# Four graph layers on one core: table writes moved to ScalarE's queue, and new times for the stages of a woven schedule

## The chip, the cores and the metric

The kernel runs on one core of a Trainium2 chip. The time is the device time of one execution in microseconds (us); smaller is better. Three runs of the kernel before gave 3189.59, 3191.43 and 3202.73 us, so the median is 3191.43 us. One more execution was taken with the hardware profiler; all durations below are from it.

Names of engines: PE is TensorE (matrix multiply; PEld is its weight load), DVE is VectorE, ACT is ScalarE, POOL is GpSimd, SP is SyncE, which here only issues DMAs. PSUM is the memory that PE writes into; SBUF is the working memory.

## What is computed

`x` is 32 items of 512 nodes with 256 features; `adj` is one 512x512 matrix with few entries that are not zero, shared by all items. Four layers follow each other. Layers 0 and 3 have the same form:

```python
pre_u = h @ W1[:d];  pre_v = h @ W1[d:]
hidden = relu(pre_u[:, :, None, :] + pre_v[:, None, :, :] + b1)
S = sigmoid(hidden @ W2 + b2)                 # one number per pair of nodes
a = einsum('buv,bud->bvd', S * adj, h)
m = einsum('uv,bud->bvd', adj, h) * h
z = beta1*h + beta2*(a @ Wa + ba) + beta3*(m @ Wm + bm)
```

Layer 1 is `z + relu((adj @ z) @ W.T + b)`. Layer 2 is a dense attention over all 512 nodes: features, one logit per node, softmax of leaky_relu(f_i + f_j) + adj, weighted sum, plus the input.

`S * adj` is zero wherever `adj` is, so the kernel computes `S` only for the pairs of nodes that have an edge.

## The kernel before, in words

The 32 items are worked in 8 groups of 4 (`NB = 4`, group number `t` = 0 to 7). For each group there are five kinds of work. Each is a Python generator, and each `yield` ends one *piece*:

- **first** (29 pieces): for each item load `x` (SP), transpose it on PE (L664) and copy it out on ACT (L665), write the transpose to DRAM (ACT's queue, L898), compute `m` on PE and DVE (`mhT`, L880) and store it (SP, L902), and then `pre`.
- **pre** (4 pieces per item, inside `first` and inside `middle`): two matmuls per piece (L678, L680) give `pre_u` and `pre_v` for 128 nodes. DVE copies one half out of PSUM with the bias (L683), ACT copies the other half (L686), DVE makes a small sum (L688). The result `puv` (128 x 512 numbers, 256 KB) is written to the group's table in DRAM (L692). `puv` has three buffers.
- **edges** (50 pieces; once for layer 0 and once for layer 3 of each group): 40 *turns*. Each turn gathers 128 rows of the table with an indirect DMA (POOL, L717), DVE combines them with the rows of the other end of the edges (L811 to L813), ACT (L797) or DVE (L831) sums them, then come exp (ACT, L702), the rest of the sigmoid and the factor `adj` (DVE), and an indirect DMA scatters the values into a dense matrix in DRAM, `cells` (POOL, L711). Four fetches run ahead of the turns, and five pieces of leftover scatters follow them.
- **middle** (about 120 pieces): load the dense `S * adj` of layer 0 (`SA`, POOL, L857), lay it out with ACT (`flat`, L944), the rest of layer 0 (L972, L979), layer 1 (L993 and `adjT,zW`), layer 2 (L1015, softmax L1039 to L1045, transposes L1084, `eT,feats`), and `pre` for layer 3. Its transposed result goes to DRAM as `x2T` (SP, L1064).
- **last** (33 pieces): for each item the products `hWa` and `mhT` of layer 3 (2 pieces each), the sums over the dense `S * adj` of layer 3 (2 pieces, L1133), the `Wm` product (2 pieces, L1142), and the store of the output (SP).

All of it is emitted into one program by `weave`. `sparse_path` gives every piece of every stream a time; one unit of time is one *turn of the groups*, and `middle` of group `t` fills the times from t - 0.47 to t + 0.53 (cut off at zero; the last two groups have some numbers of their own). `weave` sorts all pieces by time and emits them in that order, with one exception: `first` and `last` are "fill" streams. Their pieces wait in a list and are emitted only where a piece of `middle` yields True, a *room*: a place where PE would have to wait for another engine. One piece, or two if the list is long, goes into each room; more than 8 are never held back. `middle_shares` sets how much of a turn each piece of `middle` takes; so it sets which edge turns and which fill pieces come between which pieces of `middle`. PE executes nearly in the order of emission; a scheduler shifts some instructions of the other engines.

In times, a turn looks like this before the change (phase 0 is the start of a `middle`): edges of layer 3 of the group before from 0.003 to 0.54, edges of layer 0 of the group after from 0.448 to 0.96, `last` of the group before from 0.56 to 1.13, which reaches into the next turn. `first` of group t + 1 stands from 0.14 to 0.40 of the turn of group t, just before the edges of layer 0 that read its table. Group 2 is an exception: its `first` runs from 0.1 to 0.45 beside the `middle` of group 0. So the `middle` of group 1 has no `first` beside it.

The table write is held back by one piece. `pre` stores it as a closure in `self.later`, and the next piece of `pre`, of whichever stream, issues it on SP's queue through `settle`; the ends of `first` and `middle` call `settle` too:

```python
self.settle()
self.later = lambda c=c, puv=puv: nc.sync.dma_start(rows[:, c, :, b, :], puv)
yield
```

Of the kernel before, what the change touches and what calls it, by code (L numbers as in the profile page):

```python
# [19 lines left out]
NC = N // P  # L20
DC = D // P
G = 32
NB = 4
# [494 lines left out]
class Sparse:  # L518
# [3 lines left out]
    def __init__(self, ctx, m, counts, xr, outr, B):  # L522
        self.m, self.nc, self.tc, self.counts = m, m.nc, m.tc, counts
        tc = m.tc
        self.xr, self.outr = xr, outr
        pool = lambda n, b, **k: ctx.enter_context(tc.tile_pool(name=n, bufs=b, **k))
        self.dram = pool("dram", 1, space=bass.MemoryType.DRAM)

        self.cells = {
            k: [self.dram.tile([CELLS + SPARE, NB], F32, name=f"cells_{k}{q}") for q in range(2)] for k in "03"  # L530
        }
        self.lists = self.dram.tile([N, 2 * N], F32, name="lists")
        self.x2s = self.dram.tile([B, P, NC, D], F32, name="x2s")

        self.xT, self.x2T = (self.dram.tile([B, P, DC, N], F32, name=n) for n in ("xT", "x2T"))
        self.mhTs = self.dram.tile([B, P, DC, N], F32, name="mhTs")
        self.e = Edges(m, pool("edges", 1))
        self.adjT = pool("adjT1", 1).tile([P, NC, N], F32, name="adjT")
        self.grp = pool("grp", 2)
        self.act, self.small, self.gath = pool("act", 1), pool("small", 2), pool("gath", 6)  # L540
        self.ps = pool("ps", 7, space=PSUM)
        self.ps_f1 = pool("ps_f1", 1, space=PSUM)
        self.later, self.bigs, self.given, self.marks = None, 0, None, {}

    def psum(self):
        return self.ps.tile([P, N], F32, name="pst", tag="pst")
# [121 lines left out]
    def pre(self, g, b, hT):  # L668

        nc, w = self.nc, g.w  # L670
        rows = g.table.rearrange("(c p k) (b d) -> p c k b d", p=P, k=2, b=NB)
        for c in range(NC):
            cs = slice(c * P, (c + 1) * P)
            if c % 2 == 0:
                two = [self.psum() for _ in range(2)]
                for k, pp in enumerate(two):
                    ks = slice((c + k) * P, (c + k + 1) * P)
                    nc.tensor.matmul(pp, hT[:, 0, ks], w["W1"][:, 0::DC, :], start=True, stop=False)  # L678
            pp = two[c % 2]
            nc.tensor.matmul(pp, hT[:, 1, cs], w["W1"][:, 1::DC, :], start=False, stop=True)  # L680
            puv = self.small.tile([P, 2, D], F32, name="puv", bufs=3)
            part, mixed = (g.parts[:, k, c, b : b + 1] for k in range(2))
            nc.vector.scalar_tensor_tensor(  # L683
                puv[:, 0, :], pp[:, 0:D], 1.0, w["bu"], ALU.mult, ALU.add, accum_out=part
            )
            nc.scalar.copy(puv[:, 1, :], pp[:, D:])  # L686
            junk = self.small.tile([P, MIXED.stop - MIXED.start], F32, name="mixed", bufs=1)
            nc.vector.scalar_tensor_tensor(  # L688
                junk, puv[:, 0, MIXED], 1.0, w["sign"][:, 0, :], ALU.mult, ALU.mult, accum_out=mixed
            )  # L690
            self.settle()
            self.later = lambda c=c, puv=puv: nc.sync.dma_start(rows[:, c, :, b, :], puv)  # L692
            yield

    def settle(self):

        if self.later:
            self.later()
        self.later = None

    def exp_of(self, w, t):
        self.behind(self.nc.scalar.activation(t, t, AF.Exp, bias=w["nb2"], scale=-1.0))  # L702
# [182 lines left out]
    def first(self, g, i):  # L885


        def load(b):
            h = self.act.tile([P, NC, D], F32, name="h0", tag="h", bufs=2)
            self.nc.sync.dma_start(h, self.xr[i + b])  # L890
            return h

        h = load(0)
        for b in range(NB):
            ahead = load(b + 1) if b < NB - 1 else None
            hT = self.turned(h, "hT0", "hT")
            yield
            self.nc.scalar.dma_start(self.xT[i + b], hT)  # L898
            if i > 0:
                for mhT in self.mhT(h, hT, 3):  # L900
                    yield
                self.nc.sync.dma_start(self.mhTs[i + b], mhT)  # L902
            yield from self.pre(g, b, hT)
            h = ahead
        self.settle()

    def middle_before(self, g0, i):

# [14 lines left out]
    def middle(self, g0, g3, i):  # L923


        SA = self.load(g0, 0)
        given, self.given = self.given, None
        mhT, hT = self.fresh(i, given)
        hT = hT()
        hWa = None  # L930
        if not given:
            for hWa in self.hWa(g0, hT, 0):
                yield
        flat = self.flat(SA, 0)
        for b in range(NB):
            keep = [mhT, hT, hWa, flat]
            yield from self.middle_one(g0, g3, b, i + b, SA, keep, given)
            mhT, hT, hWa, flat = keep
        self.settle()

    def flat(self, SA, b):
        flat = self.act.tile([P, NC, N], F32, name="flat", tag="eT")
# [236 lines left out]
def spread(shares, a, b):  # L1179

    times, at = [], 0.0
    for share in shares:
        times.append(a + (b - a) * at / sum(shares))
        at += share
    return times


def edge_times(ahead, a, b, behind, lead=LEAD):

    step = (b - a) / TURNS  # L1190
    first = [ahead + j * min(step, (a - ahead) / lead) for j in range(lead)]
    return first + spread(even(TURNS), a, b) + spread(even(TAIL), b, behind)


def middle_shares(given):


    hWa = [] if given else [1.7, 1.7]
    shares = list(hWa)
    for b in range(NB):  # L1200
        more = hWa if b < NB - 1 else []
        shares += [3.4, 3.4, 1.0, 2.7]
        shares += [1.7, 3.4, 2.8, 4.5] + [0.9] * NC
        shares += [0.4, 0.4, 0.4, 1.0, 0.4, 1.0] + more + [1.5, 1.5]
        shares += [2.8, 4.5] + [0.4] * NC + [0.5, 0.5]
    return shares + [0.1]


@with_exitstack
def sparse_path(ctx, m, counts, xr, outr, B):  # L1210


    sp = Sparse(ctx, m, counts, xr, outr, B)
    last = B // NB - 1
    streams = [
        (sp.setup(), spread(even(NC + 1 + NC + 2 * (OWN // 2 + 1) + 1), -0.40, -0.295), ""),
        (sp.setup_behind(), spread(even(2 * (OWN // 2 + 1) + 2 * PANELS + 4), -0.285, -0.16), ""),
        (sp.setup_rest(), spread(even(8), -0.26, -0.20), ""),
        (sp.zeros_behind(), spread(even(2), 0.15, 0.2), ""),
    ]  # L1220
    for t in range(last + 1):
        g0, g3 = Group(sp, m.g0, f"0_{t}"), Group(sp, m.g3, f"3_{t}")
        start, end = (max(0.0, k - 0.47) for k in (t, t + 1))

        if t == 0:
            first = spread(even(NB * 5 + 1), -0.385, -0.30)
            edges0 = edge_times(-0.292, -0.27, -0.03, -0.02, LEAD_AT_ENDS)
        elif t == 1:
            first = spread(FIRST, -0.28, -0.06)
            edges0 = edge_times(0.02, 0.07, start - 0.06, start - 0.04)  # L1230
        else:
            first = spread(FIRST, 0.1, 0.45) if t == 2 else spread(FIRST, start - 0.86, start - 0.6)
            edges0 = edge_times(start - 0.552, start - 0.505, start - 0.06, start - 0.04)
        edges3 = edge_times(end + 0.003, end + 0.05, end + 0.48, end + 0.54)
        behind = end + 0.56, end + 1.13
        if t == last - 1:
            edges3 = edge_times(end + 0.003, end + 0.05, end + 0.46, end + 0.5)
            behind = end + 0.7, end + 1.06
        if t == last:
            end -= 0.2  # L1240
            edges3 = edge_times(end + 0.003, end + 0.02, end + 0.45, end + 0.46, LEAD_AT_ENDS)
            behind = end + 0.29, end + 0.45
        streams += [
            (sp.first(g0, t * NB), first, "fill"),
            (sp.edges(g0, ("yT", "mhT0", "hWa0") if t == 0 else ()), edges0, ""),
            (sp.middle(g0, g3, t * NB), spread(middle_shares(t == 0), start, end), "main"),
            (sp.edges(g3, ("yT", "h1", "hT1") if t == last else ()), edges3, "free"),
        ]
        if t == 0:
            streams.append((sp.middle_before(g0, 0), spread(AHEAD, -0.15, -0.03), ""))  # L1250
        if t < last:
            streams.append((sp.last(g3, t * NB), spread(LAST, *behind), "fill"))
        else:
            streams.append((sp.last_before(g3, t * NB), spread(AHEAD, *behind), ""))
            streams.append((sp.last_behind(g3, t * NB), spread(BEHIND, end + 0.5, end + 0.6), ""))
    sp.weave(streams)
# [237 lines left out]
```

## Time and profile before

| | |
|---|---|
| median of 3 runs | 3191.43 us |
| the profiled execution | 3192.99 us |
| its span, first to last instruction | 3190.9 us |
| mean granted TensorE clock | 0.933 |
| PE / DVE / POOL / ACT busy | 2746.0 / 2110.6 / 1590.5 / 1338.4 us |
| mean busy share of PEld | 52% |
| mean DMA rate | 228 GB/s |

The profiled execution lies 1.6 us above the median. A line of the profile's groups reads: source line, engine, operation, output<-inputs, shapes, count, then busy time and mean duration of one in ns, then the idle time of the engine just before these instructions and what ended it. A table by stretches gives, for each stretch of the span, the busy time of each engine with the number of instructions, then the mean granted PE clock (1.00 is full) and the DMA engines' busy share. A line of the waits reads: who waited <- for whom, total us, number of waits, longest. PE's fp32 matmuls appear as two records each.

### The profile page before, as it was taken

How to read it: one execution, taken by the hardware profiler on the slowest of the kernel's cores; microseconds unless marked ns; L12 is line 12 of the kernel's file. 1: busy time of each engine (PE TensorE's matmuls, PEld its weight loads, DVE VectorE, ACT ScalarE, POOL GpSimd, SP SyncE). 2: the span in 40 equal slices, each digit the busy share in tenths (PEclk: the TensorE clock that was granted, in tenths of full speed). 3: DMA queues.
4: the chain of work that ended last, by engine and by line, in shares of the span. 5: the costliest groups of instructions: out<-in, count | busy, mean ns of one | idle time of the engine just before them, and what ended most of it. 6: DMA issues, size and time to landing. Idle time of an engine off the chain costs nothing.

```text
span 3190.9 us, 32573 instructions
## 1 busy us (share of the span) xinstructions
PE 2746.0 (86%) x8729; PEld 1659.2 (52%) x8730; DVE 2110.6 (66%) x5601; ACT 1338.4 (42%) x4185; POOL 1590.5 (50%) x1535
## 2 busy tenths in 40 slices
PE   6756998769998898988999899998999889979948
PEld 3423444435664555545665456545655456535627
DVE  6752665877577775776767675877757775773651
ACT  4432543544344442544344443544434443443330
POOL 2562443666454564546635464546635564460360
PEclk9887998879999999999999899999999899989979
DMA  7874766677677766786578866786678766652763
GB/s 245 314 218 160 263 203 210 205 238 242 199 258 263 265 225 225 241 286 216 183 263 259 283 212 229 233 269 244 221 241 270 256 227 213 203 192 90 243 200 112
DMA packets 308607, 727.39 MB, mean 228 GB/s; under 512 B 58048, under 2 KB 161472, under 8 KB 300224
## 3 DMA queue, kind: packets, MB, share of 16 engines
q0 software_dynamic: 136128, 448.24, 43.2%
q1 hardware_dynamic: 153904, 240.30, 22.2%
q10 hardware_dynamic: 18384, 36.71, 3.1%
q8 instruction: 70, 1.15, 0.1%
q14 instruction: 121, 0.99, 0.1%
HBM read 564.28 MB, written 160.83 MB: 227 GB/s over the span
## 4 chain that ended last, share of the span: by engine, by line
PE 51%; DMA 20%; DVE 14%; issue 7%; POOL 5%; ACT 3%; POOLq 0%; ACTq 0%; DVEq 0%; SPq 0%
PE pst L49 22%; DMA rows<-table,iv 8%; PE pst L1133 5%; PE pst L678 4%; PE pst L680 4%; PE pst L972 4%; DMA cells<-s,cell 4%; DMA table<-puv 3%; DVE rows L811 3%; PE pst L993 3%; PE pst L1015 2%; POOL cells L711 2%; PE pst L1142 2%; DVE s L831 2%; DVE rows L813 2%
## 5 line engine op out<-in xcount | busy, mean ns | idle before, releaser
L711 POOL DMA_INDIRECT cells<-s,cell x640 | 716.5, 1120 | 845.3 <-DMA cells<-s,cell 524.4
L717 POOL DMA_INDIRECT rows<-table,iv x552 | 597.6, 1083 | 490.1 <-issue 142.3
L797 ACT ACTIVATE rows<-rows 128x256 f32<-128x256 f32 x1160 | 468.9, 406 | 672.7 <-DVE rows L813 359.4
L811 DVE TENSOR_TENSOR rows<-rows,mine 128x576 f32<-128x576 f32 x616 | 462.5, 751 | 324.1 <-DMA rows<-table,iv 301.6
L49 PE MATMUL pst<-adj,h 128*128 128x512 f32 x1024 | 456.0, 592 | 2.4 <-ACT puv L686 2.4
L49 PE MATMUL pst<-L_gnn_Wa,hT 128*128 128x256 f32 x1024 | 277.7, 424 | 139.9 <-DMA hT<-x2T 55.2
L831 DVE TENSOR_REDUCE s<-rows 128x4 f32<-128x1024 f32 x326 | 394.9, 1211 | 2.8
L813 DVE TENSOR_TENSOR rows<-rows,mine 128x448 f32<-128x448 f32 x616 | 379.8, 617 | 0.0
L49 PEld LDWEIGHTS pst<-L_gnn_Wa,hT 128*128 128x128 f32 x1024 | 217.3, 217 | 189.1 <-issue 49.8
L49 PEld LDWEIGHTS pst<-adj,h 128*128 128x128 f32 x1024 | 191.7, 190 | 219.9 <-issue 215.0
L49 PE MATMUL pst<-eT,feats 128*128 128x512 f32 x512 | 251.5, 648 | 31.5 <-ACT eT L1085 31.5
L683 DVE SCALAR_TENSOR_TENSOR puv<-pst,L_gnn_bu 128x256 f32<-128x256 f32 x256 | 106.2, 418 | 242.5 <-DMA table<-puv 137.1
L49 PE MATMUL pst<-adjT,zW 128*128 128x512 f32 x512 | 231.5, 604 | 15.4 <-ACT zW L997 15.4
L1133 PE MATMUL pst<-hWa,SA 128*128 128x256 f32 x896 | 218.3, 399 | 3.1 <-DMA SA<-cells 3.1
L1133 PEld LDWEIGHTS pst<-hWa,SA 128*128 128x128 f32 x896 | 213.7, 328 | 10.3 <-DMA SA<-cells 4.2
L797 ACT ACTIVATION_READ_ACCUMULATOR rows<-rows 128x1 f32 x1160 | 218.1, 188 | 0.0
L686 ACT COPY puv<-pst 128x256 f32<-128x256 f32 x256 | 92.2, 371 | 299.6 <-DVE puv L683 289.6
L944 ACT COPY flat<-SA 128x512 f32<-128x512 f32 x128 | 137.4, 1122 | 182.5 <-DMA SA<-cells 104.1
L972 PE MATMUL pst<-flat,hWa 128*128 128x512 f32 x448 | 197.9, 593 | 2.8 <-ACT hWa L870 2.8
L49 PEld LDWEIGHTS pst<-eT,feats 128*128 128x128 f32 x512 | 104.4, 208 | 163.7 <-issue 124.4
L1084 PE MATMUL pst<-ident,ex 128*128 128x128 f32 x512 | 91.0, 318 | 106.4 <-DVE ex L1045 63.6
L993 PE MATMUL pst<-WT,hT 128*128 128x256 f32 x512 | 136.4, 423 | 45.7 <-DVE hT L980 41.1
(216 smaller groups left out, 4103.5 us busy)
## 6 DMA issues: line engine op xcount, KB each, us to landing
table<-puv SPq DMA_DIRECT2D x256, 256.0 KB, 5.2
SA<-cells POOLq DMA_DIRECT2D x64, 1024.0 KB, 7.1
mine<-table SPq DMA_DIRECT2D x64, 512.0 KB, 6.3
rows<-table POOLq DMA_DIRECT2D x64, 512.0 KB, 5.2
h<-in_x_dram SPq DMA_DIRECT2D x36, 512.0 KB, 5.2
hT<-xT SPq DMA_DIRECT2D x36, 512.0 KB, 4.8
h<-x2s SPq DMA_DIRECT2D x36, 512.0 KB, 3.7
xT<-hT ACTq DMA_DIRECT2D x32, 512.0 KB, 5.3
```

The source lines that it names most:

```text
L49: nc.tensor.matmul(out, lhsT, rhs, start=(n == 0), stop=(n == len(pairs) - 1))
L678: nc.tensor.matmul(pp, hT[:, 0, ks], w["W1"][:, 0::DC, :], start=True, stop=False)
L711: self.nc.gpsimd.indirect_dma_start(out=g.cells[half], out_offset=bass.IndirectOffsetOnAxis(ap=at, axis=0), in_=s, in_offset=None)
L717: self.nc.gpsimd.indirect_dma_start(out=rows, out_offset=None, in_=g.table, in_offset=bass.IndirectOffsetOnAxis(ap=at, axis=0))
L797: self.behind(nc.scalar.activation(part, part, AF.Identity, accum_out=g.s[:, k, b : b + 1]))
L811: self.behind(nc.vector.tensor_tensor(rows[:, :, first], rows[:, :, first], other[:, :, first], ALU.max))
L813: self.behind(nc.vector.tensor_tensor(rows[:, :, behind], rows[:, :, behind], other[:, :, behind], ALU.min))
L831: nc.vector.tensor_reduce(g.s[:, k, :], rows, AX.X, ALU.add)
L944: self.nc.scalar.copy(flat[:, r, :], SA[r][:, :, b])
L972: nc.tensor.matmul(pz, hWa[:, r, cs], flat[:, r, :], start=(r == 0), stop=False)
L993: nc.tensor.matmul(pw[:, at], zT[:, d, cs], m.WT_1[:, d, :], start=(d + k == 0), stop=(d * k == 1))
L1133: nc.tensor.matmul(pz[:, k * D : (k + 1) * D], SA[r][:, cs, b], hWa[:, r, :], start=(r + k == 0), stop=False)
```

## The change

Three things change.

1. The table write is issued from ACT's queue, in the same piece as the copy, and no longer held back. `later` and `settle` go.
2. `first` of the groups 3 to 7 moves from 0.86 .. 0.6 before the group's `middle` to 1.95 .. 1.52 before it: one turn earlier, and over a longer stretch (0.43 in place of 0.26). Group 2 starts at 0.08 in place of 0.1. Groups 0 and 1 keep their times.
3. `middle_shares` and the times of edges and `last` get new numbers. In the shares, the pieces that end in a room and those of the softmax and of `pre` take more of a turn; the split of the four softmax pieces is laid out anew.

The list of items in `Edges.order` is not edited.

```diff
-            self.settle()
-            self.later = lambda c=c, puv=puv: nc.sync.dma_start(rows[:, c, :, b, :], puv)
+            nc.scalar.dma_start(rows[:, c, :, b, :], puv)
             yield
...
     for b in range(NB):
-        more = hWa if b < NB - 1 else []
-        shares += [3.4, 3.4, 1.0, 2.7]
-        shares += [1.7, 3.4, 2.8, 4.5] + [0.9] * NC
-        shares += [0.4, 0.4, 0.4, 1.0, 0.4, 1.0] + more + [1.5, 1.5]
-        shares += [2.8, 4.5] + [0.4] * NC + [0.5, 0.5]
+        more = 0.0 if given or b == NB - 1 else 1.7
+        shares += [3.4, 3.4, 1.0, 3.8]
+        shares += [1.7, 4.5, 2.7, 5.5, 0.9, 0.9, 0.9, 3.7]
+        shares += [1.5, 1.5, 1.5, 2.5, 1.5, 2.5]
+        for _ in range(2):
+            shares += [more] if more else []
+            shares += [2.5]
+        shares += [2.7, 5.5] + [1.0] * NC + [0.8, 0.8]
...
-            first = spread(FIRST, 0.1, 0.45) if t == 2 else spread(FIRST, start - 0.86, start - 0.6)
-            edges0 = edge_times(start - 0.552, start - 0.505, start - 0.06, start - 0.04)
-        edges3 = edge_times(end + 0.003, end + 0.05, end + 0.48, end + 0.54)
-        behind = end + 0.56, end + 1.13
+            first = spread(FIRST, 0.08, 0.45) if t == 2 else spread(FIRST, start - 1.95, start - 1.52)
+            edges0 = edge_times(start - 0.54, start - 0.495, start - 0.06, start - 0.04)
+        edges3 = edge_times(end + 0.003, end + 0.045, end + 0.485, end + 0.52)
+        behind = end + 0.54, end + 1.05
```

More of the change, by code (lines that the diff above doesn't have):

```diff
@@ L542, in __init__ @@
         self.ps_f1 = pool("ps_f1", 1, space=PSUM)
-        self.later, self.bigs, self.given, self.marks = None, 0, None, {}
+        self.bigs, self.given, self.marks = 0, None, {}
     def psum(self):
@@ L690, in pre @@
             )
-            self.settle()
-            self.later = lambda c=c, puv=puv: nc.sync.dma_start(rows[:, c, :, b, :], puv)
+            nc.scalar.dma_start(rows[:, c, :, b, :], puv)
             yield
[L695 to L699, printed above, removed]
     def exp_of(self, w, t):
@@ L904, in first @@
             h = ahead
-        self.settle()
     def middle_before(self, g0, i):
@@ L938, in middle @@
             mhT, hT, hWa, flat = keep
-        self.settle()
     def flat(self, SA, b):
```

## The prediction

> **What bounds the kernel now.** I read the page first: PE is busy 2746.0 of 3190.9 us, far above DVE (2110.6), so some 445 us without PE are the reserve. Then I asked for stretches cut where PE starts a `middle` and where it starts the `last` that goes with it. "Turn k" is the `middle` of group k; its first half has the edges of layer 3, its second those of layer 0.
>
> ```profile
> core 0: us, PE busy (x) PEld busy (x) DVE busy (x) ACT busy (x) POOL busy (x), PEclk, DMA share, GB/s
> 533.00:703.00 170.00, 119.11 (x344) 67.08 (x343) 123.44 (x309) 80.69 (x255) 104.43 (x93) 0.84 0.71 223
> 703.00:865.00 162.00, 144.87 (x490) 95.56 (x488) 116.60 (x283) 67.11 (x213) 93.31 (x87) 0.95 0.67 228
> ...
> 1231.00:1427.00 196.00, 189.94 (x584) 107.45 (x585) 141.05 (x389) 92.86 (x286) 96.86 (x91) 0.97 0.80 264
> 1427.00:1601.00 174.00, 146.20 (x490) 95.22 (x489) 117.10 (x283) 67.17 (x213) 102.97 (x93) 0.94 0.63 213
> ...
> 2324.00:2526.00 202.00, 189.63 (x585) 106.91 (x586) 142.09 (x391) 92.31 (x284) 99.79 (x93) 0.97 0.79 257
> 2526.00:2692.00 166.00, 145.13 (x489) 93.99 (x487) 115.93 (x282) 66.52 (x211) 97.17 (x91) 0.96 0.65 219
> ```
>
> Rows one and two are turn 1, the next two turn 3, the last two turn 6. Turns 2 to 6 look alike: a first half of 196 to 202 us in which PE is busy 188 to 190, so PE bounds it; a second half of 163 to 174 us with PE busy 146, so some 20 us of waits. Turn 1 has no `first`: its first half takes 170 us with PE busy 119, and I read 170 as what the edges alone need. PE's waits in turn 3, first half, then second:
>
> ```profile
> PE pst L49 <- ACT puv L686: 7.9, 1, 7.9
> PE pst L49 <- ACT eT L1085: 3.4, 1, 3.4
> PE pst L1084 <- DVE ex L1045: 1.8, 1, 1.8
> ```
>
> ```profile
> PE pst L49 <- ACT puv L686: 11.4, 1, 11.4
> PE pst L678 <- DVE yT L1062: 4.5, 1, 4.5
> PE pst L1084 <- DVE ex L1045: 3.7, 2, 3.3
> PE pst L993 <- DVE hT L980: 3.5, 2, 2.1
> PE pst L1133 <- DMA SA<-cells: 2.0, 1, 2.0
> ```
>
> The longest is the border between turns: ACT has a `flat` copy that waits for the last `SA` load ahead of the `puv` copies, and PE gets no PSUM tile. The softmax (ex, eT) waits where no fill piece stood in the room.
>
> **Part 1: `first` a turn earlier, `last` sooner.** The PE groups of one turn (1231 to 1600.6) price the fill:
>
> ```profile
> L49 PE MATMUL pst<-adj,h 128*128 128x512 f32 x128 | 57.2, 592 | 0.0
> ...
> L1133 PE MATMUL pst<-hWa,SA 128*128 128x256 f32 x128 | 31.4, 400 | 2.0 <-DMA SA<-cells 2.0
> ...
> L1142 PE MATMUL pst<-L_gnn_Wm,mhT 128*128 128x256 f32 x64 | 15.4, 381 | 0.4 <-DVE mhT L880 0.4
> L680 PE MATMUL pst<-w_L_gnn_W,hT 128*128 128x512 f32 x32 | 15.9, 592 | 0.0
> L678 PE MATMUL pst<-w_L_gnn_W,hT 128*128 128x512 f32 x32 | 15.0, 592 | 0.0
> ```
>
> `first` is half of row one (the other half is `last`'s) plus L678, L680 and the transposes L664 (4.1): 28.6 + 15.0 + 15.9 + 4.1 = 63.6 us of PE. `last` has eight pieces of each kind: sums 31.4/8 = 3.9, `Wm` 15.4/8 = 1.9, `mhT` 28.6/8 = 3.6, `hWa` 2.1 by its row in the same answer.
>
> The order of the two built programs shows what moves. `first` leaves turn 6 and enters turn 1; turns 2 to 5 keep one, of another group. Pieces 23 to 31 of each `last` stood in the next turn's first half; now 27 to 31 do. So 23 to 26 (1.9 + 2.1 + 2.1 + 3.6 = 9.7 us) go to the second half.
>
> - Turns 2 to 5, first half: 9.7 us less PE where PE bounds: -9.7. Bounds: 0 (edges late next) to -9.7.
> - Second half: 9.7 us more PE beside 20 us of waits. Most of those (border, yT, hT) stand where no piece goes, so I let 7 stay: +7. Bounds 0 to +9.7.
> - Turn 1, first half: PE 119.1 falls to 103 at the clock of the full turns (0.84/0.97) and rises by 63.6; with their 9.5 us of waits 176, without any clock gain 192. I take 183: +13 (bounds +6 to +22). Second half as above.
> - Turn 6, first half: no `first`; 202 becomes turn 1's 170 and a little for the 15 us of `last` left: 172, -30 (bounds -32 to -20).
> - Turn 7 (2692 to 2932): 9.7 us of PE less beside some 36 us of gaps: -3 (0 to -9.7).
>
> **Part 2: shares and edge times.** Counted in the order of turn 3: before, 12 rooms get no piece, among them the last six of `first`'s half and six in the softmax of the second; after, 4. Softmax waits are 3.4 + 1.8 + 3.7 + 0.7 = 9.6 us a turn; I let two thirds go: -6 a turn, -3 in turns 1 and 6, whose first halves are counted above (bounds 0 to -9.6). Late next is the dense load of layer 3: between the edges' last turn and the first sums of `last` PE now has about 4 us less work, while the scatters after that turn keep their length (1406 to 1457 us in turn 3). PE waited 2.0 us there; I take +2 (0 to +4).
>
> **Part 3: table writes on ACT.**
>
> ```profile
> L692 SPq DMA_DIRECT2D table<-puv x256: 512/519/1757, 46.7 to 2968.1; - x128
> ```
>
> ```profile
> table<-puv SPq DMA_DIRECT2D x256, 256.0 KB, 5.2
> ...
> x2s<-x ACTq DMA_DIRECT2D x64, 256.0 KB, 3.2
> ```
>
> SP loses 256 x 0.519 = 133 us of issuing, ACT gains it: 32 writes a turn with 0.04 us around each (as seen after x2s issues) are 18 us beside ACT's 160 of 370. The write waits for its own copy (0.37 us). Behind it in ACT's queue stand the edges' sums (L797), `flat`, `x2s`; PE waits for `flat` and for PSUM tiles. One `pre` in `middle` asks ACT for 4 copies (1.5), 4 of `flat` (4.5), two `x` copies (1.2) and two issues (0.65): 7.8 us, beside about 8.2 of PE; with four writes 10.1. PSUM's seven tiles and DVE's slack cover most: +1 a turn (bounds 0 to 8 x 2.2 = +18). At the border the order now has two `puv` copies ahead of the waiting `flat`, so 3.8 us of products can come early, but the fourth `flat` now stands behind two writes and other copies, some 4 us; I take 0 (-3.8 to +4).
>
> SP: its writes waited 458.0 us for ACT's copies, with `x2T`, `hT` and `h` behind them. PE waits for those loads only in the setup and at the end, so the relief is -2 in all. DVE waits for a free `puv` buffer 35 times, 137.1 us; with the same three buffers I leave it (0 to half).
>
> The same 256 KB land in 5.2 us from SP and 3.2 us from ACT in the rows above; if the table writes took ACT's figure, up to 35 x 2.0 = 70 us of DVE's waits would go, none of it on PE's path: nothing in the sum. A rule of the Trainium skill speaks against even that ("DMA: Bandwidth & Descriptors", section "Issuing engines are not separate DMA queues"): all issuers end on the same 16 DMA engines, and spreading the issues saves only the sequencer's own time, usually small. By the rule the writes land no sooner than before, and the sum is 3162 us as well.
>
> **The sum.** Turns 2 to 5: 4 x (-9.7 + 7 - 6 + 2 + 1) = -22.8. Turn 1: 13 + 7 - 3 + 2 + 1 = +20. Turn 6: -30 + 7 - 3 + 2 + 1 = -23. Turn 7 -3, setup -2. Together -30.8. The profiled execution took 3192.99 us (span 3190.9), 1.6 above the median 3191.43: **3162 us**, 0.9% below that median. About 0.5%, 16 us, is what a measurement can tell from no change here.
>
> **Rivals.** *More* (3120): the second half takes its 9.7 us for nothing, so the 7 goes in six turns: 42 us below 3162. For: it has 20 us of waits. Against: these stand at fixed places (border, yT, hT, dense load), where no fill piece is emitted. *No change* (3190): the second half pays all 9.7 and the dense load 4, so a full turn gains 1 (four: -4), turn 1 loses 25, turn 6 gains 18, turn 7 and the setup -5: -2 in all. For: the work is the same and turns 1 and 6 only trade places. That is also the case where the title promises more than the edit: the items' order is untouched. *Slower* (3232): ACT becomes late in `middle`'s `pre`. Place: `flat` and the copies that free PSUM, 32 times; price 4 x 0.56 = 2.2 us each, 70 us on 3162. It decides from the point where ACT's 10.1 us are not covered by PE's 8.2 and the free PSUM tiles. For: PE already waits for `puv` copies at each border. Against: ACT is busy 42%.
>
> **How the numbers follow.** Forecast 0.38 (3145 to 3175), more 0.20, no change 0.22, slower 0.20. Faster by over 0.5%: 0.38 + 0.20 = 0.58; within 0.22; slower 0.20. The range 3110 to 3225 cuts half of the slower case and a third of *more*: 0.17 left out.
>
> **What would show it.** PE busy in turn 1's first half up to some 175 us at a clock near 0.97, turn 6's down to about 120 at 0.84; first halves of turns 2 to 5 near 188; waits for ex and eT down by two thirds; the dense-load wait (L1133) at 2 to 4 us a turn. Wrong would be: waits for `flat` or `puv` copies at every `pre`, not only at the border; or first halves still at 198, which says that the edges and not PE set them.

## The result, and the profile after

The changed kernel takes **3226.66 us** (median, 3214.35 to 3229.43), the kernel before 3189.59 us beside it (3180.3 to 3202.73). The ratio is 1.0107, 95% interval 1.0084 to 1.0131: 1.1% slower, where 0.9% faster was forecast. The profiled execution has a span of 3226.9 us, 36.0 above that of before.

PE's work has not grown. The line of the engines on the changed kernel's page (busy us, share, instructions):

```profile
PE 2733.9 (85%) x8729; PEld 1644.5 (51%) x8730; DVE 2113.9 (66%) x5601; ACT 1345.6 (42%) x4185; POOL 1588.0 (49%) x1535
```

PE is busy 12.1 us less than before (2746.0) and the span is 36.0 longer. So PE's idle time, span less busy, went from 444.9 to 493.0 us: **all of the loss is new waiting of PE**. Lines of the changed kernel carry smaller numbers: the table write L692 is L691, the lines behind it are 7 less, and 8 or 9 less from the end of `first` on (the `puv` copy stays L686, `hWa` L870 is L863, `flat` L944 is L935, the first product of `middle` L972 is L963).

The tables by stretches below are cut at the first product of each `middle` (L972, after L963) and at the first of each `last`. The prediction's rows begin 4 to 7 us earlier, at the `hWa` products, so lengths are compared within these two tables alone. Columns are as in the prediction's (stretch, length, then PE, PEld, DVE, ACT and POOL busy, clock, DMA share, GB/s). Before, both halves of turn 3:

```profile
1238.00:1427.00 189.00, 183.39 (x568) 102.13 (x568) 140.25 (x384) 88.39 (x277) 96.86 (x91) 0.98 0.80 265
1427.00:1607.00 180.00, 152.20 (x506) 100.03 (x505) 117.91 (x288) 71.05 (x220) 102.97 (x93) 0.92 0.63 213
```

After, first half of turn 1, both halves of turn 3, first half of turn 6:

```profile
546.00:722.00 176.00, 161.82 (x481) 84.22 (x482) 135.67 (x375) 87.68 (x272) 100.68 (x91) 0.97 0.83 273
1276.00:1463.00 187.00, 177.12 (x536) 96.70 (x537) 139.88 (x380) 88.54 (x272) 92.02 (x88) 0.96 0.79 258
1463.00:1647.00 184.00, 154.40 (x538) 101.52 (x536) 119.03 (x292) 71.87 (x227) 101.39 (x96) 0.95 0.66 220
2385.00:2552.00 167.00, 130.77 (x376) 75.36 (x377) 122.30 (x302) 77.33 (x241) 95.86 (x86) 0.87 0.68 220
```

The reader is to see turns 1 and 6 change places: the first half of turn 1 went from 166 to 176 us and that of turn 6 from 197 to 167, about as forecast. The full turns lose. On the mean of turns 2 to 5, the first half went from 191.8 to 186.4 us with PE busy 5.8 us less, and the second from 173.0 to 184.3 us with PE busy only 3.9 us more: 7.4 us of that growth are waiting.

With boundaries taken at the first product of each `middle` and of each `last`, turns 2 to 5 last 374.0, 370.7, 367.9 and 370.1 us, before 367.5, 368.9, 361.1 and 361.3: 6.0 more each. Which waits these are, the list of PE's waits tells (who waited <- for whom, total, number, longest), cut 3 us after the start of turn 2 and of turn 7, so that five turns and five borders are in it: 873 to 2702 us before, 905 to 2744 after. The lines for the softmax and the border, before, then after:

```profile
PE pst L1084 <- DVE ex L1045: 38.3, 13, 5.1
PE pst L49 <- ACT puv L686: 30.5, 5, 11.4
```

```profile
PE pst L963 <- ACT hWa L863: 77.2, 5, 16.4
PE pst L678 <- DVE yT L1053: 26.5, 5, 8.1
PE pst L984 <- DVE hT L971: 22.8, 11, 5.6
PE pst L1075 <- DVE ex L1036: 21.5, 12, 5.7
```

The first line of after is new in size (2.8 us in all before): five waits, one at each border between turns, up to 16.4 us each. Before, the border's wait was the `puv` line. ACT's part of the timeline of the changed kernel at the border of turns 3 and 4 shows it (start, duration, engine, line, operation; in brackets the idle time before and what ended it):

```profile
1629.74 0.53 ACTq L691 DMA_DIRECT2D table<-puv  x1
1642.21 1.09 ACT L935 COPY flat<-SA 128x512 f32<-128x512 f32 x1 [12.50 <-DMA SA<-cells]
...
1646.33 0.59 ACT L863 COPY hWa<-pst 128x512 f32<-128x512 f32 x1
...
1647.32 1.10 ACT L935 COPY flat<-SA 128x512 f32<-128x512 f32 x1
```

Two `puv` copies (1628.32 and 1629.34) do come ahead of the waiting `flat`, as the order had shown; the table writes go out behind them. PE gets its tiles, does `hWa` at once, is out of work at 1630.7 and stands until 1647.0. The third `flat` copy waits for the third `SA` load, and seven copies and issues more stand behind it before the `hWa` copy. Before, PE waited for `puv` first and did `hWa` after. The wait was not taken away but moved behind `hWa`, and it grew, because the third `SA` load now comes later: 26.9 us on the mean of turns 2 to 7, 18.5 before, counted from the start of the edges' last turn on DVE (L811; the expectations below call it the edges' last multiply).

### The profile page after: what moved, and what is told of

Its sections match the earlier page's. It is cut to its first block, busy times and chain, and to the rows that moved or that the text cites. A ratio compares the mean times of both kernels' runs of the same rounds, so it can differ in the third digit from the quotient of the medians.

```text
span 3226.9 us, 32527 instructions
## 1 busy us (share of the span) xinstructions
PE 2733.9 (85%) x8729; PEld 1644.5 (51%) x8730; DVE 2113.9 (66%) x5601; ACT 1345.6 (42%) x4185; POOL 1588.0 (49%) x1535
## 5 line engine op out<-in xcount | busy, mean ns | idle before, releaser
L704 POOL DMA_INDIRECT cells<-s,cell x640 | 705.4, 1102 | 896.3 <-DMA cells<-s,cell 555.6
L710 POOL DMA_INDIRECT rows<-table,iv x552 | 618.7, 1121 | 412.0 <-issue 106.9
L49 PE MATMUL pst<-L_gnn_Wa,hT 128*128 128x256 f32 x1024 | 262.3, 409 | 100.6 <-DMA hT<-x2T 51.0
L963 PE MATMUL pst<-flat,hWa 128*128 128x512 f32 x448 | 211.6, 628 | 89.9 <-ACT hWa L863 89.9
L49 PEld LDWEIGHTS pst<-L_gnn_Wa,hT 128*128 128x128 f32 x1024 | 207.7, 208 | 149.8 <-issue 53.2
L49 PE MATMUL pst<-eT,feats 128*128 128x512 f32 x512 | 232.8, 608 | 19.4 <-ACT eT L1076 19.4
L935 ACT COPY flat<-SA 128x512 f32<-128x512 f32 x128 | 135.9, 1119 | 243.7 <-DMA SA<-cells 191.6
L686 ACT COPY puv<-pst 128x256 f32<-128x256 f32 x256 | 94.4, 370 | 293.9 <-DVE puv L683 268.9
L963 PEld LDWEIGHTS pst<-flat,hWa 128*128 128x128 f32 x448 | 88.2, 202 | 195.5 <-issue 95.8
L971 DVE TENSOR_TENSOR hT<-hT,pst 128x512 f32<-128x512 f32 x64 | 43.5, 681 | 213.6 <-PE pst L970 213.6
L49 PEld LDWEIGHTS pst<-eT,feats 128*128 128x128 f32 x512 | 97.6, 194 | 144.7 <-issue 114.6
```

Source lines behind the costliest of these rows:

```text
L49: nc.tensor.matmul(out, lhsT, rhs, start=(n == 0), stop=(n == len(pairs) - 1))
L704: self.nc.gpsimd.indirect_dma_start(out=g.cells[half], out_offset=bass.IndirectOffsetOnAxis(ap=at, axis=0), in_=s, in_offset=None)
L710: self.nc.gpsimd.indirect_dma_start(out=rows, out_offset=None, in_=g.table, in_offset=bass.IndirectOffsetOnAxis(ap=at, axis=0))
L935: self.nc.scalar.copy(flat[:, r, :], SA[r][:, :, b])
L963: nc.tensor.matmul(pz, hWa[:, r, cs], flat[:, r, :], start=(r == 0), stop=False)
```

## The experiments

My theory from the two traces was that the new times put PE's work where the edges' two runs and the two turn-arounds between them set the turn (theory B in the expectations); the rival was the queue of the table writes (theory A). Ratios are against the kernel before, timed beside each kernel on the same chip. "PE idle" is span less PE busy of the profiled execution, "border" PE's waits for `puv` (L686) and `hWa` (L870), cut at turns 2 and 7 as above.

| kernel | median us | ratio (95%) | PE idle | border |
|---|---|---|---|---|
| before | 3189.6 | 1 | 444.9 | 33.3 |
| changed | 3226.7 | 1.0107 (1.0084-1.0131) | 493.0 | 83.8 |
| e1 writes on ACT alone | 3204.2 | 1.0047 (1.0023-1.0070) | 455.5 | 41.3 |
| e2 `first` alone | 3235.6 | 1.0144 (1.0110-1.0178) | 494.5 | 35.8 |
| e3 shares alone | 3253.4 | 1.0198 (1.0167-1.0228) | 511.7 | 90.1 |
| e4 windows alone | 3178.4 | 0.9970 (0.9951-0.9989) | 437.3 | 24.1 |
| e5 changed, writes as before | 3223.0 | 1.0098 (1.0073-1.0124) | 481.0 | 62.2 |
| e6 changed, `first` as before | 3238.7 | 1.0146 (1.0121-1.0170) | 494.5 | 78.0 |
| e7 changed, shares as before | 3188.2 | 0.9985 (0.9967-1.0003) | 445.0 | 34.3 |
| e8 window of `last` alone | 3175.1 | 0.9953 (0.9936-0.9970) | 430.6 | 18.1 |
| e9 windows of edges alone | 3192.5 | 1.0019 (1.0000-1.0039) | 440.0 | 24.2 |
| e10 `first` ahead, same phase | 3218.3 | 1.0079 (1.0055-1.0103) | 471.1 | 38.6 |
| e11 e3, last writes held | 3243.3 | 1.0170 (1.0143-1.0197) | 485.6 | 57.2 |
| e12 changed, last writes held | 3215.4 | 1.0087 (1.0061-1.0112) | 478.2 | 75.2 |
| e13 new shares, last item only | 3231.0 | 1.0136 (1.0107-1.0166) | 493.8 | 80.1 |
| e14 new shares, items 0 to 2 | 3196.8 | 1.0026 (1.0008-1.0045) | 445.2 | 28.4 |
| e15 changed, last item old | 3205.5 | 1.0067 (1.0039-1.0095) | 455.0 | 34.3 |
| e16 e8 with `first` ahead | 3194.1 | 1.0017 (0.9988-1.0046) | 457.9 | 23.2 |

PE's busy time lies between 2733.9 and 2756.8 in all of them; the idle column makes the time.

**One part at a time** (e1 to e4). Each is the kernel before with the lines of one part of the diff: e1 the write in `pre` (and no `settle`), e2 the line of `first` for groups 3 to 7 and the 0.08, e3 the body of `middle_shares`, e4 the three lines of `edges0`, `edges3` and `behind`.

> The kernel before with one part of the change alone: the table writes issued from ScalarE's queue right after their copy; times, shares and windows stay those of before. Theory A (the border between turns, +6.5 us six times, and the gap between the two runs of edges, +5 us six times, grew because flat and hWa copies now stand behind table writes in ACT's queue): slower by 30 to 60 us than before, the border wait of PE ends on a flat or hWa copy and not on puv. Theory B (the new times put PE's work where the edges' two runs and the two turn-arounds set the turn; the writes' queue matters little): within 10 us of before.

> The kernel before with first of a group a whole turn ahead alone; nothing else changed. Both theories: turn 1 longer by 15 to 25 us, turn 6 shorter by 20 to 32, turns 2 to 5 within 3 us each, so the sum is between -12 and +5 us. If it alone is slower by over 10 us, both theories miss something about where first is emitted.

> The kernel before with the new shares of the middle stage's pieces alone; windows, first and the queue of the writes stay. Theory A: the softmax rooms get fill, waits for ex and eT fall by half and more, so 10 to 35 us faster. Theory B: a piece of the middle moved against the edges' turns only moves a wait, within 10 us of before, or slower where the last pieces before the border come earlier and the border grows.

> The kernel before with the new windows of the edges and of last alone (last 4 pieces a turn sooner, the edges' lead and tail as in the changed kernel). Theory A: first halves shorter by up to 9.7 us, second halves longer by up to 9.7, the edges' turns unchanged: within 5 us or faster by up to 20. Theory B: the gap between the edges' runs and the border grow by 3 to 6 us each in six turns while PE's share of the first half has nothing to give: slower by 20 to 45 us, with border and gap read from the last multiply of one run of edges to the fourth turn of the next.

Measured: +14, +45, +63 and -12 us. Theory A said -12 rightly for e4, but the writes on ACT cost far less than it had, with the border wait still on `puv`, and the shares cost where it had a gain. Theory B came near with e1 (its interval is 7 to 22 us) and had named a growing border as one outcome of e3, without a size; it falls with e4, which has the larger gap between the two runs of edges (6 to 10 us in place of 3.7) and is faster all the same. The shares and `first` are the costly parts; a cost of `first` neither theory had. The parts sum to +110 and together give +37, so they don't add.

In e2 turns 1 and 6 trade about as expected (turn 1 361.0 from 333.3, turn 6 343.5 from 369.8), but the first halves of turns 2 to 5 grew from a mean of 191.8 to 204.9, with no more PE work. In turn 3's run of layer-3 edges, DVE stands longer for gathered rows, before and in e2:

```profile
DVE rows L811 <- DMA rows<-table,iv: 16.5, 2, 13.8
```

```profile
DVE rows L811 <- DMA rows<-table,iv: 33.2, 3, 16.1
```

and PE has a wait of 10.0 us for `ex` and 6.8 for `hT`, both made by DVE.

**One part left out** (e5 to e7), and e10:

```diff
-            first = spread(FIRST, 0.1, 0.45) if t == 2 else spread(FIRST, start - 0.86, start - 0.6)
+            first = spread(FIRST, 0.1, 0.45) if t == 2 else spread(FIRST, start - 1.86, start - 1.6)
```

> The changed kernel with the table writes back on SP's queue behind the next copy (as before); all new times stay. Measured so far beside the kernel before: writes alone +14 us, first alone +45, shares alone +63, windows alone -12, all four together +37. Theory A (the writes on ACT make the loss of the whole): falls to within 8 us of before. Theory C (the loss is in the new times: shares at the border, first's pieces in the first half): still 15 to 37 us slower than before, with borders of 47 to 50 us and gaps of 8 to 9 us as in the changed kernel.

> The changed kernel with first's pieces at the times of before; writes, shares and windows stay new. If the costs of the parts add up: 45 us below the changed kernel, so 8 us faster than before. If first's pieces only cost where the windows of last are the old ones (both kinds crowd the same rooms): within 12 us of the changed kernel, so 25 to 45 slower than before.

> The changed kernel with the old shares of the middle stage; writes, first and windows stay new. If the border's growth comes from the shares: borders of turns 2 to 6 back from 48 to 50 us to 42 to 46, and 25 to 60 us below the changed kernel, so 20 us faster than before to 10 slower. If the border grows from the writes on ACT or from first: within 10 us of the changed kernel.

> The kernel before with first a whole turn ahead and nothing else, but in the same part of the turn as before (0.14 to 0.40 of it, where the changed kernel spreads it over 0.05 to 0.48). If first's loss of 9 us in each first half of turns 2 to 5 comes from the wider window: these halves go back to their length before, turn 1 +18 to +27, turn 6 -23 to -30, so within 12 us of before. If it comes from being a turn ahead (its loads, xT and tables of a later group): 30 to 50 us slower, as first alone was.

Without the writes on ACT the loss stays (1.0098): theory A fell, the new times make it. Without the new shares it is gone (e7, 0.9985, its interval takes in 1): **the shares are the part that costs**, 63 us alone and some 38 within the whole. `first` a turn ahead, which alone costs 45, gains some 12 within the whole (e6 is 12 slower than the changed kernel). e10 lies between its two outcomes: 26 us slower. If the two add, the wider window makes about 19 of the 45 and being a turn ahead the rest; but the first halves of turns 2 to 5, where the expectation has the loss, hardly come back (202.7 us; 204.9 in e2, 191.8 before). DVE's wait for gathered rows is there too (31.5 us). Why DVE waits longer for them was not found.

**What lengthens the border** (e11, e12). The third `SA` load waits for the last scatters (L711). POOL's timeline at one border, kernel before, then e3:

```profile
1581.29 0.99 POOL L711 DMA_INDIRECT cells<-s,cell  x1 [2.79 <-DMA cells<-s,cell]
1585.62 0.97 POOL L711 DMA_INDIRECT cells<-s,cell  x1 [3.33 <-DMA cells<-s,cell]
...
1593.74 1.14 POOL L857 DMA_DIRECT2D SA<-cells  x2 [1.46 <-DMA cells<-s,cell]
```

```profile
1612.39 1.01 POOL L711 DMA_INDIRECT cells<-s,cell  x1 [7.51 <-DMA cells<-s,cell]
...
1624.08 0.97 POOL L711 DMA_INDIRECT cells<-s,cell  x1 [7.04 <-DMA cells<-s,cell]
1628.47 1.14 POOL L857 DMA_DIRECT2D SA<-cells  x2 [3.42 <-DMA cells<-s,cell]
```

A scatter waits for the one ahead of it to land: up to 3.3 us before, 7.5 and 7.0 us for two of the last three in e3. While they ran, before moved 57 GB/s (1582 to 1594 us), since the `puv` copies stood behind `flat` and no table was written. In e3 the copies are early, and four table writes, the loads of `mine` that wait for them and an `x2s` store ran beside the scatters: 198 and 146 GB/s from 1612 to 1629. The third `SA` load comes 30.5 us after the edges' last turn in e3, against the 18.5 of before. The wait that I wanted gone had kept the DMA engines clear. The test holds back the writes of the last item of a `middle`, all but its first (e11's edit; in e12 the other writes stay on ACT's queue):

```diff
-            self.later = lambda c=c, puv=puv: nc.sync.dma_start(rows[:, c, :, b, :], puv)
+            if hold and c > 0:
+                self.held.append((rows[:, c, :, b, :], puv))
+            else:
+                self.later = lambda c=c, puv=puv: nc.sync.dma_start(rows[:, c, :, b, :], puv)
...
         SA = self.load(g0, 0)
+        for at, puv in self.held:
+            self.nc.gpsimd.dma_start(at, puv)
+        self.held = []
```

> The shares part alone (63 us slower than before) with one edit: of the last item of a middle, the table writes of the last three chunks go out from GpSimd's queue behind the SA loads of the next middle, where they and the loads of mine that wait for them can't run beside the last scatters. Theory C1 (the border grew because these transfers, now earlier, make each of the last scatters land in 7 to 8 us in place of 3, and the SA load waits for them): SA load 19 to 23 us after the edges' last multiply in place of 30, borders 42 to 46, so 20 to 40 us below the shares part. Theory C2 (the border grew because PE and ACT reach it with less work, and the scatters' rate is their own): borders stay at 48 to 51 and the time within 10 us of the shares part or, with later tables, above it.

> The changed kernel with the same edit as the run before. Theory C1: SA load 20 to 24 us after the edges' last multiply in place of 27, borders 44 to 47 in place of 49, 10 to 35 us below the changed kernel. Theory C2: within 8 us of the changed kernel or above it.

In e11 the third `SA` load came at 19 to 20 us in three borders and at 25 to 28 in the other three, and PE's border waits fell from 90.1 to 57.2 us. In the three early ones the longest wait of a scatter fell to 5.3 to 5.9 us; in the other three one still waits 7.1 to 7.5 us, so something else slows them too. So the transfers do lengthen the border of the shares part, in half of its cases. But the time fell by 10 us only, as theory C2 allows, and the two intervals overlap. The first gathers of the next run, which read these tables, came 11 to 19 us after the start of `middle` in place of 5 before it, and the layer-3 runs of edges grew from 161 to 164 us.

In e12 the `SA` load moved only from 27 to 26 us, where C1 had 20 to 24, and the border waits from 83.8 to 75.2. The time fell by 11 us by the medians and 6 by the ratios, whose intervals overlap. So C1 is not shown for the changed kernel, and POOL's timeline at its border of turns 3 and 4 says why; the first `SA` load, before, then the first and the third, after:

```profile
1574.71 0.59 POOL L857 DMA_DIRECT2D SA<-cells  x1
```

```profile
1618.42 0.57 POOL L850 DMA_DIRECT2D SA<-cells  x1
...
1636.64 1.14 POOL L850 DMA_DIRECT2D SA<-cells  x2 [4.31 <-DMA cells<-s,cell]
```

From the first `SA` load to the third it takes 18.2 us here and 19.0 before; on the mean of six borders 18.7 and 17.6, against 25.4 in e3. The chain of scatters between them is hardly slower in the changed kernel. What is late there is the first load: 8.2 us after the start of the edges' last turn, 0.9 before. This goes with the new shares of the last item (5.1 in e3, 5.6 in e13 below; 0.1 in e7 and -0.4 in e15, which have its old ones). How those shares delay it was not followed.

**The windows** (e8, e9): `last` alone and the edges alone.

```diff
-        behind = end + 0.56, end + 1.13
+        behind = end + 0.54, end + 1.05
```

> The kernel before with one window of the windows part alone: last from 0.54 to 1.05 of its turn (0.56 to 1.13 before); the edges keep their times. In the windows part the layer-3 edges' runs fell by 13 us, those of layer 0 rose by 5, the gap between them rose from 3.7 to 7 to 10 and the border by 1. If last alone gives the fall (PE's 9.7 us fewer in the first half) and the edges' windows the larger gap: first runs 145 to 150, gap 3.7, second runs 160 to 165, 15 to 40 us faster than before. If the gap comes with last's pieces: gap 7 and more, within 12 us of the windows part, so 0 to 20 faster than before.

> The kernel before with the edges' new windows alone; last keeps 0.56 to 1.13. If last's pieces are what shortens the first run: first runs stay at 158 to 162, gap 7 to 10, so 10 to 35 us slower than before. If the edges' windows themselves shorten it: 0 to 15 faster.

The window of `last` carries the gain: the first halves of turns 2 to 5 fall from 191.8 to 186.1, the second grow from 173.0 to 177.5. That is e8's first outcome, though its gain of 12 us is just short of the 15 expected. The gap between the runs of edges stays at 3.7 us in e8 and grows to 6 to 10 in e9, so it comes from the edges' windows. It costs hardly anything (+5 us, between e9's two outcomes), while the first run gets 3 us shorter. e8 is **the fastest version** measured (e4's interval overlaps its own): 0.9953 of before, and faster than the changed kernel by 1.6% (3175.1 against 3226.7).

**Which item's shares** (e13 to e16). The new shares (`new`) of some items in place of the old (`one`), scaled so that each item keeps its length; e13's edit, where e14 and e15 have `b < NB - 1`:

```diff
+        if b == NB - 1:
...
+            one = [x * sum(one) / sum(new) for x in new]
```

> The kernel before with the new shares for the last item of each middle alone (scaled to the length that the item had); items 0 to 2, windows, first and writes as before. Border theory (the loss of the shares is the last pieces next to the border): 35 to 65 us slower than before, PE's waits for hWa at the border 12 to 18 us each as with all new shares. Room theory (the loss is in how fill and rooms meet in all items): a quarter of the 63, 5 to 25 us slower, border waits below 10.

> The kernel before with the new shares for items 0 to 2 of each middle, scaled in the same way; the last item keeps the old ones. Border theory: within 15 us of before, border waits on puv of 6 to 11 us as before. Room theory: 35 to 55 us slower.

> The changed kernel with the old shares for the last item of each middle, the new ones (scaled) for items 0 to 2. Border theory: border waits fall from 15 to 16 us to below 8, 25 to 45 us below the changed kernel. Room theory: within 12 us of the changed kernel.

> The version with last's new window alone (12 to 15 us faster than before) with first a whole turn ahead added. With first alone on the old window the time rose by 45 us; within the changed kernel first gained 12. If the crowding of first and last in the same rooms was what cost: within 10 us of last's window alone, so up to 25 faster than before. If first's wide window costs wherever the old shares are: 25 to 45 us slower than last's window alone.

The border theory held in e13 and e14. The last item alone costs 43 us (1.0136), the other three 8. PE's waits in turns 2 to 6, e13, then e15:

```profile
PE pst L972 <- ACT hWa L870: 77.9, 5, 17.9
PE pst L1084 <- DVE ex L1045: 37.4, 12, 5.8
```

```profile
PE pst L1006 <- DVE yT L995: 31.6, 6, 7.9
PE pst L49 <- ACT zW L988: 30.8, 6, 7.6
...
PE pst L963 <- ACT hWa L863: 23.8, 5, 5.2
```

e13 has the long border wait and the old softmax waits (38.3 before). Putting the last item's old shares back into the changed kernel brings the border waits down to 34.3 us, but the time by 21 us only by the medians and 13 by the ratios, short of the 25 expected and close to the 12 of the room theory; part comes back as waits for `yT` and `zW`. e16 lies between its two outcomes: `first` a turn ahead costs 19 us on e8 as well; turn 6 is 22.2 shorter and turn 1 32.6 longer than in e8.

## Why the prediction was wrong, step by step

- **PE bounds the kernel, its idle time is the reserve: right.** The idle column moves with the time.
- **`first` enters turn 1 and leaves turn 6: right in size.** First half of turn 1: +9.9 (forecast +13; PE is busy 161.8 us there, not 175), of turn 6: -29.7 (forecast -30).
- **Pieces 23 to 26 leave the first half: right in kind.** First halves of turns 2 to 5: -5.4 (forecast -9.7, bounds 0 to -9.7). e8, with this part alone, gives -5.7. They fell from 191.8 to 186.4 by one cut, nearly as much as PE's work in them (5.8), with PE idle 8 to 9 us in both: PE and not the edges set them.
- **The border at 0 (-3.8 to +4): the step that failed.** It was weighed as two `puv` copies that come ahead of `flat`, for 3.8 us of early products, against some 4 us of copies and writes behind `flat`. Both came: the products are early, and from the third `flat` to the `hWa` copy it takes 4.1 us (1642.21 to 1646.33). But the time of the `SA` load was taken as it was, and behind the early products PE needs what stands behind `flat`: `flat` ends the chain scatters, `SA` load, ACT's queue. PE's border waits went from 33.3 to 83.8 us in five borders: +10.1 a turn. I asked which wait goes, and not which wait comes next on that engine. The step also stood under the wrong part: with the writes alone (e1) the border waits are 41.3 us, with the last item's new shares alone (e13) 80.1.
- **Softmax waits -6 a turn: failed.** Waits for `ex`, `eT` and `cols` fell from 55.0 to 45.1 us in five turns, -2.0 a turn, and waits for `yT` (L678, L680, L1015) rose from 23.8 to 46.3, +4.5 a turn. With the shares alone (e3) the softmax waits are 57.3 us and those for `yT` 22.5: the shares gave no relief, and what moved the waits in the whole was not isolated. That a fill piece put into one room leaves another empty is my reading, not tested; I had priced only the rooms that got one.
- **Second half +7: too low for the whole, too high for its part.** +11.3 in turns 2 to 5 (173.0 to 184.3), with the border wait's +10.1 in it; e8, which moves these pieces alone, gives +4.5. +12.9 and +15.8 in turns 1 and 6.
- **Dense load +2: right.** Waits of L1133 for `SA` and, with the same products, of the last products for `mhT`: 5.0 to 15.6 us in five turns, +2.1 a turn.
- **Writes on ACT +1 a turn: right in size within the whole.** e5 against the changed kernel: 4 us in all, no more than their intervals. Alone (e1) they cost 14 us in all. The forecast -2 of the setup did not come: in e1 the layer-0 edges of group 1 end 6 us later, in the changed kernel 9. That the writes make this is not shown, for in e3, which leaves them on SP, these edges end 5 us later too.
- **Rivals.** *Slower* gave 3232 for ACT being late with `flat` and the copies at all 32 items. The time came near, its mechanism didn't: ACT is late at the borders alone, five waits of 15 us, and what ends them is the `SA` load ahead of it. *No change* had turns 1 and 6 as a trade and missed the border.

By turns: 2 to 5 +23.9 (forecast -22.8), turn 1 +22.8 (+20), turn 6 -13.9 (-23), turn 7 to the end -6.0 (-3), before turn 1 +9.0 (-2). That is the 36 us.

Left open: why DVE waits longer for gathered rows when `first` is a turn ahead, how the last item's shares delay the first `SA` load, why the parts together cost less than their sum, and where the rest of the shares' cost goes (of some 10 us a turn in e3, the stretch from the last turn of one run of edges to the fourth turn of the next takes 6).

## What to carry to other kernels

When an edit lets a copy overtake a waiting one, follow the consumer to its next need: the gain is real only if the load behind the wait comes earlier too. A stall can keep the DMA engines clear for a chain of small dependent scatters; ending it can put large transfers beside that chain (e3 shows it, the changed kernel hardly). And time windows tuned together are tested one by one: here one line of the windows held all of the gain and one item's shares most of the loss.

## What the runs showed of the hardware

A long wait of PE costs some more than it lasts. The stretches of the changed kernel around the border of turns 3 and 4 (PE idle from 1630.7 to 1647.0):

```profile
1632.00:1638.00 6.00, 0.00 (x0) 0.00 (x0) 0.53 (x5) 0.00 (x0) 1.47 (x3) 0.75 0.43 98
...
1648.00:1652.00 4.00, 4.00 (x6) 1.67 (x5) 0.00 (x0) 1.84 (x3) 3.08 (x4) 0.50 0.88 280
1652.00:1656.00 4.00, 4.00 (x10) 1.71 (x9) 0.00 (x0) 0.00 (x0) 3.04 (x4) 0.99 1.02 412
```

The clock (the number ahead of the DMA share) falls to 0.50 some 4 us into the idle time, as the mean of 0.75 in the first row gives (3 us at 1.00, 3 at 0.50, from 1632 on), and stays there until 1652, 5 us after PE resumes. The first 16 matmul records of this `middle` (L963) took 9.66 us, against 7.03 for the same 16 of another item, from 2541.87 on, at a clock of 1.00. So an estimate from these rows is that the wait costs some 2.5 us more than it lasts. The border wait of before, 11.4 us, has it too (0.50 to 0.52 from 1596 to 1606). The Trainium skill states the rule behind it ("TensorE: Matmul & The Clock Gate", section "Part 1: The HAM clock gate (the "warmup" mystery)"): half clock after an idle window of about 3.4 us, full clock again after as much sustained work. The rows agree in kind; the drop 4 us after the last product and the return 5 us after the first are both somewhat later than that figure. Short waits seldom pay: in turns 2 to 6 of the changed kernel the clock drops in 2 of PE's 24 idle stretches of 1 to 3 us, and in all 12 of over 5 us.

The table writes landed in 4.3 us from ACT's queue in the changed kernel and 5.2 from SP's before, but in 5.3 with e1, which moves them alone, and in 4.5 from SP's queue with e5, which has the new times. So the difference goes with the new times, all taken together, and not with the queue that issues the writes (e2, e3 and e4, with one part of them each, have 5.1 to 5.7).
